# Softmax sums inverted once each through DRAM instead of as a 16-fold copy in SBUF, and down weights loaded in 11 pieces

## The chip, the core and the metric

The kernel runs on one core of a Trainium2 chip. The time is the device time of one execution in microseconds. Of three executions of the kernel before, the median is 1223.92 us (1220.72 to 1224.61).

## What is computed

One transformer layer, for 2 sequences of 1024 rows of 512 numbers, all in float32:

```
Q, K, V = x Wq^T + bq, x Wk^T + bk, x Wv^T + bv     # 32 query heads, 8 key/value heads, 16 wide
Q, K = rope(Q), rope(K)
w    = softmax(Q K^T / 4)                            # four query heads share one key head
x    = layernorm(x + (w V) Wo^T + bo)
h    = silu(x gate_w^T * gate_s) * (x up_w^T * up_s) # 1408 wide
x    = layernorm(x + (h down_w^T) * down_s)
```

What matters here is the division in the softmax. The kernel never divides the weights. It sums exp(score) x V and exp(score) over the keys, and at the end multiplies the first by the inverse of the second.

## The kernel before, in words

**Units, half-steps, iterations.** The attention is cut into 32 units (`UNITS`): one sequence, one half of 512 queries, and one key head g with its four query heads. Eight units (g from 0 to 7) make a quarter, q = 0 to 3. A unit has eight half-steps, one for each 128 keys. The loop over c (L698) does two half-steps per iteration, so a unit is four iterations and a quarter is 32; c runs from 0 to 127. Each iteration does, for the half-steps 2c and 2c+1:

- "A" products (`max_pass`, L340): scores of a unit that comes 12 half-steps later, for whose row maxima VectorE (DVE) reduces each bank (L356, eight in an iteration). `max_rows` (L359) then turns a unit's maxima, at the end of every iteration c = 1 modulo 4, with four small DVE operations and six DMAs by way of DRAM.
- "B" products (`exp_pass`, L378): the scores again, less the maxima, of which ScalarE (ACT) takes the exponential (L391, eight in an iteration).
- "V" products (`av`, L396): probabilities by V, where V is laid out with a column of ones beside each of its columns. So the accumulated result holds, for each of the four heads, sixteen rows of weighted values and, between them, sixteen equal rows of the sum of the weights.
- "F", at the head of an iteration, if there is some: one piece of other TensorE work from the list `fill`. That is first the projections of Q, K and V (up to iteration 20), and from then on the output projection and the feed-forward of the quarter before: two pieces `project` (L483), two `x1_turn` (L509), 22 `hidden` (L521) and four `down` (L568). `quarter` (L623) lists these 30 and gives the iteration `first` from which they may start.

The order of the products in an iteration is written out by hand in three lists: WITH_FILL (L683), NO_FILL (L686) and NO_A (L689, after the last A product). The order of instructions is the program's order on every engine. The products share seven banks of PSUM, handed out in turn.

**Hooks.** Before each V product `v_hook` (L692) runs what `after(k, f)` (L206) put off by k half-steps. `early` (L203) does the same at the head of an iteration. A piece that waits at a hook holds up all that comes behind it on its engine.

**The end of a unit.** `unit_out` (L413) runs with a unit's last V product, in the iteration after its last half-step. ScalarE copies the bank to `o`; two DMAs take the rows of values to `num` (L426) and the rows of sums to `den` (L427). Two units, with g even and odd, fill one `num` and one `den` of 128 rows. When the odd one is in, DVE inverts `den` in four strips of 128x128 (L432) and multiplies `num` by it (L437). For g = 7 this is placed at the next hooks, since the output projection of that quarter starts at iteration 32(q + 1) + 3; for other pairs it is placed two to four iterations later.

**The down weights.** Weights are rounded during the first 19 iterations and kept in a DRAM tensor `wsd`. The 11 slices of the down weights are fetched in one DMA at iteration 26 (L752), ahead of the first feed-forward weights and residuals. They are first read by `down`, at the end of the first quarter's feed-forward.

**The last quarter.** In quarters 0 and 1 the loop at L718 takes two pieces of `fill` in one slot where they would not all fit before the next quarter begins. Of quarter 2 two downs are kept (L770) and mixed with the projections of quarter 3 behind the loop. For the last quarter (`LASTQ`) the residuals come into a pool of five buffers (`fp5`), each when an output row of the quarter before has been stored (L597).

**The SP queue.** All DMAs are issued by SyncE (SP), in the order of the program. A DMA whose data isn't there yet holds up those behind it: KS, QH and QL of a later unit (`prep`, L325), the feed-forward weights `wt` (`ask_weights`, L458), the maxima's round trip.

Of the kernel before, what the change touches and what calls it, by code (L numbers as in the profile page):

```python
# [7 lines left out]
F32 = mybir.dt.float32  # L8
# [3 lines left out]
ALU = mybir.AluOpType  # L12
# [4 lines left out]
P = 128  # L17
B, T, D = 2, 1024, 512
HQ, HKV, HD = 32, 8, 16
G = HQ // HKV  # L20
E = 32
# [3 lines left out]
NF = INTER // P  # L25
# [3 lines left out]
HALF = 512  # L29
NH = T // HALF  # L30
# [9 lines left out]
QS = HKV * US  # L40
RING = 5
PIECES = 3 * NF
# [4 lines left out]
def attn_ffn_kernel(tc, x, wqkv, bqkv, wo, bo, rope, wg, wu, wd, gs, us, ds, out):  # L47
    nc = tc.nc

    def pool(name, bufs=1, **kw):  # L50
        return tc.alloc_tile_pool(name=name, bufs=bufs, **kw)
# [3 lines left out]
    dram2 = pool("dram2", 2, space=DRAM)  # L55
    ap1 = pool("ap1")
    ap2 = pool("ap2", 2)
# [20 lines left out]
    def leave(what):  # L78
        free.extend(held.pop(what, ()))
# [82 lines left out]
    wsd = dram.tile([PIECES, P, D], F32, name="wsd")  # L162
# [18 lines left out]
    def piece_round(i):  # L181
        w = SW.pop(i)
        SR[i] = sp4.tile([P, D], F32R, tag="sr", name="sr")
        nc.scalar.copy(SR[i], w)

        nc.vector.scalar_tensor_tensor(
            low, w.bitcast(I32), LOW, low, ALU.bitwise_and, ALU.bitwise_or
        )

    def piece_store(i):  # L190
        nc.sync.dma_start(out=wsd[i], in_=SR.pop(i).bitcast(F32))
# [8 lines left out]
        after(4, lambda: nc.vector.tensor_reduce(flag, flr, AX.X, ALU.max))  # L200

    later = {}
    early = {}  # L203
    now = [0]

    def after(n, f):  # L206
        later.setdefault(now[0] + n, []).append(f)
# [151 lines left out]
    def max_rows(u):  # L359


        neg = ap2.tile([P, TH, G], F32, tag="neg", name="neg")
        nc.vector.tensor_reduce(neg, MX.pop(u), AX.X, ALU.max, negate=True)
        mm = ap2.tile([P, G, 2, TH], F32R, tag="mm", name="mm")
        hi, lo = (mm[:, :, i, :].rearrange("p j t -> p t j") for i in range(2))
        nc.vector.tensor_copy(hi, neg)
        nc.vector.tensor_tensor(lo, neg, hi.bitcast(F32), ALU.subtract)
        mr = ap2.tile([P, E], F32, tag="mr", name="mr")
        nc.vector.transpose(mr, mm.bitcast(F32).rearrange("p j i t -> p (j i t)"))
        md = dram2.tile([E, P], F32, tag="md", name="md")  # L370
        for k in range(P // E):
            nc.sync.dma_start(out=md[:, k * E : (k + 1) * E], in_=mr[k * E : (k + 1) * E, :])
        rows = md.rearrange("(j i t) n -> i j (t n)", j=G, i=2)
        for i in range(2):
            nc.sync.dma_start(out=mts[u % 2][i : P : E, :].bitcast(F32), in_=rows[i])
# [16 lines left out]
            leave(("B", n, j))  # L392

    PV, PVN, NUM = {}, {}, {}

    def av(n, prob):  # L396
        u, kc = divmod(n, US)
# [15 lines left out]
    def unit_out(u):  # L413


        b, qh, g = UNITS[u]
        q = u // HKV
        o = ap1.tile([P, HALF], F32, tag="o", name="o")
        nc.scalar.copy(o, PV.pop(u))  # L419
        if g % 2 == 0:  # L420
            NUM[q, g // 2] = ap4.tile([P, HALF], F32, tag="num", name="num")
            NUM["den"] = ap1.tile([P, HALF], F32, tag="den", name="den")
        num, den = NUM[q, g // 2], NUM["den"]
        r0 = (g % 2) * G * HD
        rows = slice(r0, r0 + G * HD)
        nc.sync.dma_start(out=num[rows, :], in_=o[0:P:2, :])  # L426
        nc.sync.dma_start(out=den[rows, :], in_=o[1:P:2, :])  # L427
        if g % 2:
            c = now[0] // 2
            for k in range(TH):  # L430
                ns = slice(k * P, (k + 1) * P)
                f = lambda ns=ns: nc.vector.reciprocal(den[:, ns], den[:, ns])  # L432
                if g == HKV - 1:
                    after(k // 2 + 1, f)
                else:
                    early.setdefault(c + 2 + k // 2, []).append(f)
            f = lambda: nc.vector.tensor_tensor(num, num, den, ALU.mult)  # L437
            if g == HKV - 1:
                after(3, f)
            else:  # L440
                early.setdefault(c + 4, []).append(f)


    XQ, FP = {}, {}
    DONE = set()
    LASTQ = B * NH - 1

    def load_residual(q, t):
        b, qh = divmod(q, NH)
# [33 lines left out]
    def project(q, t):  # L483
        py = bank("py")
        for c in range(NC):
# [6 lines left out]
            )  # L492
        if q == LASTQ:
            row = XQ[q, t]
# [26 lines left out]
    def hidden(q, f, up):  # L521
# [13 lines left out]
        if not up:  # L535
            if f == 0:
# [8 lines left out]
            after(  # L545
                1 if q == LASTQ else 2,
                lambda: nc.vector.scalar_tensor_tensor(z, th, 1.0, z, ALU.add, ALU.mult),
# [4 lines left out]
        pus = FP["tmp"].tile(  # L552
            [P, HALF], F32, tag="pus" if q == LASTQ else "th", name="pus"
        )
        nc.scalar.mul(pus, p, ust[:, f : f + 1])  # L555

        def rest():
            nc.gpsimd.tensor_tensor(z, pus, z, ALU.mult)  # L558
            if q == LASTQ:
                nc.scalar.copy(hi, z)  # L560
# [7 lines left out]
    def down(q, t, f0=0, f1=NF):  # L568
# [14 lines left out]
        ys = fp1.tile([P, D], F32, tag="ys", name="ys")  # L583
        if q == LASTQ:
            nc.vector.tensor_tensor(ys, pd, dsb, ALU.mult)
# [8 lines left out]
        def store():  # L594
# [4 lines left out]
            for i in range(TH):  # L599
                if (q + 1, i) not in XQ and q < LASTQ and (q + 1, i) not in DONE:  # L600
                    if i <= t + (q + 1 == LASTQ):
# [19 lines left out]
    fill = [(0, f) for f in fill]  # L621

    def quarter(q):  # L623
        first = (q + 1) * QS // 2 + 3
        fs = [lambda t=t: (project(q, t), project(q, t + 1)) for t in (0, 2)]
        fs += [lambda t=t: (x1_turn(q, t), x1_turn(q, t + 1)) for t in (0, 2)]
        for f in range(NF):
            for up in (0, 1):
                fs.append(lambda a=(q, f, up): hidden(*a))
        downs = [(t, 0, NF) for t in range(TH)]  # L630
        if q == LASTQ:

            downs[:2] = [(0, 0, NF - 1), (1, 0, NF - 1), (0, NF - 1, NF), (1, NF - 1, NF)]
        for a in downs:
            fs.append(lambda a=a: down(q, *a))
        return [(first, f) for f in fs]
# [55 lines left out]
    def v_hook(n):  # L692
        now[0] = n
        for f in later.pop(n, ()):
            f()

    before = None
    for c in range(STEPS // 2):  # L698
        probs = {}

        pieces = [i for i in (2 * c - 4, 2 * c - 3) if 0 <= i < PIECES]
        for i in pieces:
            piece_round(i)
        if pieces:
            after(1, lambda ps=pieces: [(piece_store(i), piece_load(i + 4)) for i in ps])
        for f in early.pop(c, ()):
            f()
        alone = 2 * c + LEAD >= STEPS
        has_fill = bool(fill) and fill[0][0] <= c
        if c >= (STEPS - QS) // 2:  # L710
            has_fill = has_fill and len(fill) > 2
        for s in NO_A if alone else WITH_FILL if has_fill else NO_FILL:
            if s == "F":
                if has_fill:
                    fill.pop(0)[1]()
                    leave("F")

                    while c < (STEPS - QS) // 2 and (rest := len(fill) % PHASES) and QS // 2 - 1 - c % (QS // 2) < rest < DOWNS:  # L718
                        fill.pop(0)[1]()
                        leave("F")  # L720
                continue
            n = 2 * c + int(s[-1])
            if s[0] == "V":
                v_hook(n)
                if before is not None:
                    av(n - 2, before[n - 2])
                continue
            j, i = int(s[1]), "abc".index(s[2])
            if s[0] == "A":
                max_pass(n + LEAD, j, i)  # L730
                continue
            if i == 2 and n not in probs:
                probs[n] = ap3.tile([P, G, HALF], F32, tag="prob", name="prob")
            exp_pass(n, j, i, probs.get(n))
        before = probs
        u, s = divmod(2 * c + 1, US)
        if s == US - 1 and u + 3 < len(UNITS):
            prep(u + 3)
        if (2 * c + 1 + LEAD) % US == US - 1 and not alone:
            max_rows((2 * c + 1 + LEAD) // US)  # L740
        if c == QS // 2 - 10:
            low_flag()
        if c == QS // 2 - 6:
            sp4.release()
            qp4.release()
            qp2.release()
            qp1.release()
            fp1 = pool("fp1", side="right")
            fp2 = pool("fp2", 2, side="right")
            fp5 = pool("fp5", 5, side="right")  # L750
            wd_sb = fp1.tile([P, NF, D], F32R, name="wd_sb")
            nc.sync.dma_start(  # L752
                out=wd_sb.bitcast(F32), in_=wsd[2 * NF : PIECES].rearrange("f p n -> p f n")
            )
            FP["tmp"] = fp1
            ask_weights(RING - 1)
            for t in range(TH):
                load_residual(0, t)
            for q in range(B * NH - 1):
                fill.extend(quarter(q))  # L760
# [15 lines left out]
    n = 2 * STEPS  # L776
# [137 lines left out]
```

## Time and profile before

| what | value |
|---|---|
| median of three executions | 1223.92 us |
| the profiled execution | 1221.5 us, its span 1219.6 us |
| mean granted TensorE clock | 0.971 |
| DVE L356, reductions to maxima | 1024 of 682 ns |
| DVE L432, reciprocals 128x128 | 64, 893/896/954 ns (least, median, most) |
| DVE L437, num by den | 16 of 682 to 1158 ns |
| DMAs num<-o, den<-o | 32 each, 128 KB each |
| DMA wd_sb<-wsd | 1, 2816 KB, issued at 301.8 us |

The profile is that of one execution. "Busy" is the time in which an engine had an instruction in work; instructions that issue DMAs are not counted as busy. A busy TensorE is not TensorE at its peak. The chain of waits is followed back from the last instruction, at each step to what released it. The windows of the loop are named by their time in us from the start of the span. Their last columns are the granted TensorE clock (1.00 is full), the mean busy share of the 16 DMA engines and GB/s. In rows in order of time, the columns are the start, the duration, the engine (SPq is SP's queue) and the line; "[x <-y]" is idle time of the engine before the row, and what ended it.

### The profile page before, as it was taken

How to read it: one execution, taken by the hardware profiler on the slowest of the kernel's cores; microseconds unless marked ns; L12 is line 12 of the kernel's file. 1: busy time of each engine (PE TensorE's matmuls, PEld its weight loads, DVE VectorE, ACT ScalarE, POOL GpSimd, SP SyncE). 2: the span in 40 equal slices, each digit the busy share in tenths (PEclk: the TensorE clock that was granted, in tenths of full speed). 3: DMA queues.
4: the chain of work that ended last, by engine and by line, in shares of the span. 5: the costliest groups of instructions: out<-in, count | busy, mean ns of one | idle time of the engine just before them, and what ended most of it. 6: DMA issues, size and time to landing. Idle time of an engine off the chain costs nothing.

```text
span 1219.6 us, 22668 instructions
## 1 busy us (share of the span) xinstructions
PE 1159.8 (95%) x8784; PEld 599.9 (49%) x8784; DVE 872.3 (72%) x1492; ACT 702.7 (58%) x1300; POOL 352.4 (29%) x340
## 2 busy tenths in 40 slices
PE   7799999999999999999999999999899999999896
PEld 5344444444443554545444454446444454554585
DVE  4568898878877788876577878885758878742434
ACT  2016767656645677775445777774537777774251
POOL 3116362440103122223512222224412222226431
PEclk9769999999999999999999999999989999999899
DMA  5366877442611222222202222221312232111240
GB/s 162 105 190 223 271 244 252 148 175 61 202 45 62 80 80 80 80 85 65 88 28 88 80 80 80 80 80 53 114 37 75 85 95 81 46 54 53 95 122 37
DMA packets 82290, 126.80 MB, mean 104 GB/s; under 512 B 15873, under 2 KB 29442, under 8 KB 82050
## 3 DMA queue, kind: packets, MB, share of 16 engines
q1 hardware_dynamic: 82178, 125.30, 32.5%
q8 instruction: 71, 1.16, 0.4%
q14 instruction: 41, 0.34, 0.1%
HBM read 80.43 MB, written 36.44 MB: 96 GB/s over the span
## 4 chain that ended last, share of the span: by engine, by line
PE 72%; DVE 16%; POOL 4%; DMA 4%; issue 2%; ACT 1%; SPq 0%; POOLq 0%; DVEq 0%; ACTq 0%
PE pa L348 17%; PE pv L403 16%; PE pg L527 13%; PE pb L383 12%; DVE mx L356 8%; PE pq L256 5%; PE pd L574 4%; PE py L486 3%; DVE den L432 2%; DVE st L471 1%; POOL xq L591 1%; POOL ys L590 1%; ACT prob L391 1%; DMA den<-o 1%; POOL xq L481 1%
## 5 line engine op out<-in xcount | busy, mean ns | idle before, releaser
L356 DVE TENSOR_REDUCE mx<-pa 128x1 f32<-128x512 f32 x1024 | 644.6, 682 | 183.3 <-PE pa L348 130.5
L391 ACT ACTIVATE prob<-pb 128x512 f32<-128x512 f32 x1024 | 542.1, 600 | 239.9 <-PE pb L383 206.6
L348 PE MATMUL pa<-KS,QH 32*128 32x512 f32 x1024 | 361.2, 469 | 18.5 <-DVE mx L356 10.2
L348 PE MATMUL pa<-KS,QL 32*128 32x512 f32 x1024 | 336.3, 427 | 0.0
L383 PE MATMUL pb<-QH,KS 32*128 32x512 f32 x1024 | 309.4, 464 | 20.2 <-DVE mx L356 13.6
L383 PE MATMUL pb<-QL,KS 32*128 32x512 f32 x1024 | 277.5, 421 | 0.0
L403 PE MATMUL pv<-prob,va 128*32 128x512 f32 x2048 | 276.9, 612 | 0.0
L383 PE MATMUL pb<-mt,ones 32*128 32x512 f32 x1024 | 251.9, 403 | 0.0
L348 PEld LDWEIGHTS pa<-KS,QH 32*128 32x128 f32 x1024 | 155.7, 188 | 178.1 <-DVE mx L356 120.1
L558 POOL TENSOR_TENSOR z<-pus,z 128x512 f32<-128x512 f32 x44 | 56.3, 1279 | 445.4 <-ACT pus L555 418.3
L348 PEld LDWEIGHTS pa<-KS,QL 32*128 32x128 f32 x1024 | 167.1, 189 | 29.1 <-issue 19.0
L383 PEld LDWEIGHTS pb<-QL,KS 32*128 32x128 f32 x1024 | 131.2, 185 | 87.8 <-issue 85.8
L383 PEld LDWEIGHTS pb<-QH,KS 32*128 32x128 f32 x1024 | 131.0, 184 | 62.1 <-DVE mx L356 42.2
L527 PE MATMUL pg<-x1h,wt 128*128 128x512 f32 x352 | 146.3, 416 | 0.7 <-ACT x1h L516 0.7
L383 PEld LDWEIGHTS pb<-mt,ones 32*128 32x128 f32 x1024 | 138.5, 185 | 3.3
L527 PE MATMUL pg<-x1l,wt 128*128 128x512 f32 x352 | 139.2, 396 | 0.3 <-DVE x1l L517 0.3
L403 PEld LDWEIGHTS pv<-prob,va 128*32 128x32 f32 x2048 | 41.1, 108 | 94.2 <-issue 83.5
L527 PEld LDWEIGHTS pg<-x1h,wt 128*128 128x128 f32 x352 | 67.1, 191 | 38.0 <-issue 11.7
L256 PE MATMUL pq<-xT,wqkv_sb 128*128 128x512 f32 x160 | 77.9, 634 | 1.3 <-DVE mx L356 1.3
L527 PEld LDWEIGHTS pg<-x1l,wt 128*128 128x128 f32 x352 | 67.2, 191 | 12.8 <-DVE x1l L517 0.8
L574 PE MATMUL pd<-wd_sb,hh 128*128 128x512 f32 x176 | 69.9, 397 | 0.7 <-ACT o L419 0.7
L574 PE MATMUL pd<-wd_sb,hl 128*128 128x512 f32 x176 | 68.6, 390 | 0.0
(80 smaller groups left out, 968.9 us busy)
## 6 DMA issues: line engine op xcount, KB each, us to landing
wt<-wsd SPq DMA_DIRECT2D x88, 256.0 KB
KS<-kT SPq DMA_DIRECT2D x128, 128.0 KB
wsd<-sr SPq DMA_DIRECT2D x33, 256.0 KB
qT<-hi SPq DMA_DIRECT2D x16, 512.0 KB
qT<-lo SPq DMA_DIRECT2D x16, 512.0 KB
QH<-qT SPq DMA_DIRECT2D x32, 256.0 KB
QL<-qT SPq DMA_DIRECT2D x32, 256.0 KB
xs<-in_x_dram SPq DMA_DIRECT2D x16, 256.0 KB
```

The lines of the kernel that those rows point to most:

```text
L256: nc.tensor.matmul(pq, wqkv_sb[:, c, m * P : (m + 1) * P], XT[b, half][:, c, :], start=c == 0, stop=c == NC - 1,)
L348: nc.tensor.matmul(PA[n, j], (QH, QL)[i][u][r, t * P : (t + 1) * P], KS[u][r, half * HALF : (half + 1) * HALF], start=i == 0, stop=i == 1,)
L356: nc.vector.tensor_reduce(MX[u][:, t, j, half : half + 1], PA.pop((n, j)), AX.X, ALU.max)
L383: nc.tensor.matmul(PB[n, j], ones[r, :] if i == 2 else KS[u][r, kc * P : (kc + 1) * P], (QH[u], QL[u], mts[u % 2])[i][r, :], start=i == 0, ...
L391: nc.scalar.activation(prob[:, j, :], PB.pop((n, j)), AF.Exp, scale=SCALE)
L403: nc.tensor.matmul(PV[u][j * E : (j + 1) * E, :], vas[b][:, kc, g, :, :].rearrange("p d o -> p (d o)"), prob[:, j, :], start=done == 0, st ...
L432: f = lambda ns=ns: nc.vector.reciprocal(den[:, ns], den[:, ns])
L471: nc.vector.bn_stats(st, row)
L486: nc.tensor.matmul(py, NUM[q, c][:, t * P : (t + 1) * P], wo_sb[:, c, :], start=c == 0, stop=c == NC - 1,)
L527: nc.tensor.matmul(p, w[:, c, :], x1[:, c, :], start=c == 0 and k == 0, stop=c == NC - 1 and k == 1,)
L558: nc.gpsimd.tensor_tensor(z, pus, z, ALU.mult)
L574: nc.tensor.matmul(pd, h[:, f, t * P : (t + 1) * P], wd_sb[:, f, :], start=f == 0 and k == 0, stop=f == NF - 1 and k == 1,)
```

## The change

For all units but the last two (g = 6 and 7 of the last quarter, which keep the old way), `den` is no longer copied from `o` and inverted as it lies. Of the sixteen equal rows of each head one is stored to DRAM (`sd`, 4 x 512). From there 128 rows of 16 numbers are loaded (`rc`), DVE inverts these 2048 numbers once, they are stored to DRAM again (`rd`), and four DMAs spread each head's row over its sixteen rows of `den`. The stages follow each other by k half-steps: the load k after the unit's end, the inversion 2 later (k + 2), the spreading at 2k + 2, and for odd g the multiplication of `num` at 3k + 2. k is 1 for g = 7 and otherwise 2. All of them stand at hooks; `early` is gone.

The feed-forward of a quarter may start at iteration 32(q + 1) + 4 instead of + 3. The down weights are fetched in 11 DMAs of one slice, one at the end of each iteration from c = 36 to 46, instead of one DMA at c = 26.

```diff
--- before.py
+++ after.py
@@ -200,7 +200,6 @@
         after(4, lambda: nc.vector.tensor_reduce(flag, flr, AX.X, ALU.max))
 
     later = {}
-    early = {}
     now = [0]
 
     def after(n, f):
@@ -392,6 +391,7 @@
             leave(("B", n, j))
 
     PV, PVN, NUM = {}, {}, {}
+    LASTQ = B * NH - 1
 
     def av(n, prob):
         u, kc = divmod(n, US)
@@ -424,26 +424,45 @@
         r0 = (g % 2) * G * HD
         rows = slice(r0, r0 + G * HD)
         nc.sync.dma_start(out=num[rows, :], in_=o[0:P:2, :])
+        if q < LASTQ or g // 2 < HKV // 2 - 1:
+
+            sd = dram2.tile([G, HALF], F32, tag="sd", name="sd")
+            rd = dram2.tile([G, HALF], F32, tag="rd", name="rd")
+            rc = ap2.tile([P, G * HALF // P], F32, tag="rc", name="rc")
+            flat = "j (p n) -> (j p) n"
+            nc.sync.dma_start(out=sd, in_=o[1:P:E, :])
+
+            def inverse():
+                nc.vector.reciprocal(rc, rc)
+                nc.sync.dma_start(out=rd.rearrange(flat, n=G * HALF // P), in_=rc)
+
+            def spread():
+                for j in range(G):
+                    nc.sync.dma_start(
+                        out=den[r0 + j * HD : r0 + (j + 1) * HD, :],
+                        in_=rd[j : j + 1, :].to_broadcast([HD, HALF]),
+                    )
+
+
+            k = 1 if g == HKV - 1 else 2
+            after(k, lambda: nc.sync.dma_start(out=rc, in_=sd.rearrange(flat, n=G * HALF // P)))
+            after(k + 2, inverse)
+            after(2 * k + 2, spread)
+            if g % 2:
+                after(3 * k + 2, lambda: nc.vector.tensor_tensor(num, num, den, ALU.mult))
+            return
         nc.sync.dma_start(out=den[rows, :], in_=o[1:P:2, :])
         if g % 2:
-            c = now[0] // 2
             for k in range(TH):
                 ns = slice(k * P, (k + 1) * P)
-                f = lambda ns=ns: nc.vector.reciprocal(den[:, ns], den[:, ns])
-                if g == HKV - 1:
-                    after(k // 2 + 1, f)
-                else:
-                    early.setdefault(c + 2 + k // 2, []).append(f)
-            f = lambda: nc.vector.tensor_tensor(num, num, den, ALU.mult)
-            if g == HKV - 1:
-                after(3, f)
-            else:
-                early.setdefault(c + 4, []).append(f)
+                after(
+                    k // 2 + 1, lambda ns=ns: nc.vector.reciprocal(den[:, ns], den[:, ns])
+                )
+            after(3, lambda: nc.vector.tensor_tensor(num, num, den, ALU.mult))
 
 
     XQ, FP = {}, {}
     DONE = set()
-    LASTQ = B * NH - 1
 
     def load_residual(q, t):
         b, qh = divmod(q, NH)
@@ -621,7 +640,7 @@
     fill = [(0, f) for f in fill]
 
     def quarter(q):
-        first = (q + 1) * QS // 2 + 3
+        first = (q + 1) * QS // 2 + 4
         fs = [lambda t=t: (project(q, t), project(q, t + 1)) for t in (0, 2)]
         fs += [lambda t=t: (x1_turn(q, t), x1_turn(q, t + 1)) for t in (0, 2)]
         for f in range(NF):
@@ -703,8 +722,6 @@
             piece_round(i)
         if pieces:
             after(1, lambda ps=pieces: [(piece_store(i), piece_load(i + 4)) for i in ps])
-        for f in early.pop(c, ()):
-            f()
         alone = 2 * c + LEAD >= STEPS
         has_fill = bool(fill) and fill[0][0] <= c
         if c >= (STEPS - QS) // 2:
@@ -738,6 +755,8 @@
             prep(u + 3)
         if (2 * c + 1 + LEAD) % US == US - 1 and not alone:
             max_rows((2 * c + 1 + LEAD) // US)
+        if 0 <= (f := c - QS // 2 - 4) < NF:
+            nc.sync.dma_start(out=wd_sb[:, f, :].bitcast(F32), in_=wsd[2 * NF + f])
         if c == QS // 2 - 10:
             low_flag()
         if c == QS // 2 - 6:
@@ -749,9 +768,6 @@
             fp2 = pool("fp2", 2, side="right")
             fp5 = pool("fp5", 5, side="right")
             wd_sb = fp1.tile([P, NF, D], F32R, name="wd_sb")
-            nc.sync.dma_start(
-                out=wd_sb.bitcast(F32), in_=wsd[2 * NF : PIECES].rearrange("f p n -> p f n")
-            )
             FP["tmp"] = fp1
             ask_weights(RING - 1)
             for t in range(TH):
```

## The prediction

> **What bounds the kernel now.** I read the page first, then the chain of waits, then the loop cut into iterations (each runs from the first V product of one iteration to that of the next), then DVE's and SP's rows in order of time.
>
> ```profile
> PE 1159.8 (95%) x8784; PEld 599.9 (49%) x8784; DVE 872.3 (72%) x1492; ACT 702.7 (58%) x1300; POOL 352.4 (29%) x340
> ...
> PE 72%; DVE 16%; POOL 4%; DMA 4%; issue 2%; ACT 1%; SPq 0%; POOLq 0%; DVEq 0%; ACTq 0%
> PE pa L348 17%; PE pv L403 16%; PE pg L527 13%; PE pb L383 12%; DVE mx L356 8%; PE pq L256 5%; PE pd L574 4%; PE py L486 3%; DVE den L432 2%; DVE st L471 1%; POOL xq L591 1%; POOL ys L590 1%; ACT prob L391 1%; DMA den<-o 1%; POOL xq L481 1%
> ```
>
> On average TensorE bounds, but a sixth of the chain is DVE: reductions (L356) and 2.4% (29 us) reciprocals (L432). Where DVE matters is told only by iteration. Windows of iterations 48 to 52, with feed-forward work in each (columns: window, length, then busy us and instructions of PE, PEld, DVE, ACT, POOL):
>
> ```profile
> 469.70:476.90 7.20, 7.20 (x69) 3.65 (x65) 5.07 (x9) 5.48 (x11) 3.14 (x3) 1.00 0.53 176
> 476.90:484.10 7.20, 7.20 (x70) 3.67 (x66) 6.58 (x14) 5.34 (x10) 0.04 (x1) 1.00 0.06 22
> 484.10:492.40 8.30, 7.82 (x71) 3.71 (x67) 7.48 (x12) 5.10 (x10) 3.13 (x3) 1.00 0.22 67
> 492.40:499.80 7.40, 7.40 (x70) 3.74 (x66) 6.72 (x12) 5.38 (x10) 0.04 (x1) 1.00 0.30 79
> 499.80:507.00 7.20, 7.20 (x72) 3.67 (x71) 5.09 (x9) 5.52 (x11) 3.12 (x3) 1.00 0.50 164
> ```
>
> 7.2 us is TensorE's pace (eight pg products take 2.04, the attention part about 5.15). Only the window with three of the four reciprocals is longer, by 1.1, the next by 0.2: DVE is late, banks stay full, TensorE waits. Iterations 30 to 35, the first four without such work, the last two with a projection of 7.08 us:
>
> ```profile
> 325.20:331.00 5.80, 5.80 (x61) 2.99 (x63) 5.19 (x9) 3.84 (x8) 0.00 (x0) 1.00 0.03 6
> 331.00:336.70 5.70, 5.70 (x59) 2.92 (x56) 5.09 (x9) 4.06 (x9) 0.00 (x0) 1.00 0.00 0
> 336.70:342.50 5.80, 5.80 (x62) 2.96 (x59) 5.20 (x9) 4.63 (x10) 0.00 (x0) 1.00 0.67 208
> 342.50:351.40 8.90, 6.76 (x63) 2.96 (x60) 8.20 (x13) 4.64 (x9) 0.00 (x0) 0.99 0.04 15
> 351.40:365.90 14.50, 14.50 (x79) 6.35 (x76) 7.66 (x16) 4.24 (x8) 0.00 (x0) 0.89 0.02 3
> 365.90:378.80 12.90, 12.59 (x79) 5.20 (x75) 7.81 (x15) 4.24 (x8) 5.76 (x6) 1.00 0.27 83
> ```
>
> A plain iteration is DVE's: eight reductions of 0.682 with 0.04 between them give 5.76, against 5.15 that TensorE needs. There every DVE microsecond counts in full: iteration 33, with the four reciprocals, is 3.1 longer, and the first projection is 1.6 longer than the second.
>
> **Reciprocals out.** 64 of 896 ns become 4 (the last pair keeps its own) and 30 of 128x16. One small one is not in the trace: an eighth of 896 is 0.11; the 128x16 cast and subtraction take 0.18 and 0.20; 0.11 + 0.20 is the upper end. I take 0.2, 0.24 with its gap. DVE's busy time falls by 60 x 0.896 - 30 x 0.2 = 48 to about 824, but it counts only as follows.
>
> - Feed-forward iterations, eight pairs: windows 41-43, 49-51, 57-59, 73-75, 81-83, 89-91, 105-107, 113-115 lie above three times 7.18 by 1.33, 1.35, 1.35, 1.34, 1.33, 1.35, 1.34 and 1.71, together 11.1. The new work (a small one in each iteration c = 2 mod 4, the product of 0.68 in every eighth) leaves DVE below 7.18: all of it is gained. A ninth pair (1076 to 1085 us) meets no more reductions: nothing.
> - Iterations with projections of Q, K, V (TensorE 8.78): pairs at 9-11 and 17-19 cost 1.7 and 0.24. The first product moves to iteration 12, where DVE already has 8.8 of 8.92: -0.5. Gain 1.4.
> - Plain iterations 21 to 34, two pairs: 8 x 0.936 = 7.5, less four small ones, 1.0: 6.5.
> - The turns at 65 and 97: four reciprocals 3.75, less one small: 3.5 each, 7.0.
>
> **The four transfers.** For a group's last unit they are one half-step apart (about 2.1 and 3.6 us in turn), otherwise two. Durations come from SP's rows and the chain:
>
> ```profile
> 272.75 1.72 SPq L372 DMA_DIRECT2D md<-mr  x4
> 275.53 1.15 SPq L375 DMA_DIRECT2D mt<-md  x2
> 278.74 0.34 SPq L198 DMA_DIRECT2D fl<-red  x1
> 286.05 0.23 SPq L199 DMA_DIRECT2D flr<-fl  x1
> ```
> ```profile
> 341.44 2.86 DMA den<-o
> 344.32 1.76 DVE den L432 x2
> ```
>
> Before, den landed 2.86 after its issue, and DVE waited 0.67 for it. The nearest rows to the 64-byte pieces are md<-mr (128-byte pieces; the read-back was issued 1.1 after the last write) and fl<-red (4-byte pieces: 7.3). The Trainium skill, "DMA: Bandwidth & Descriptors" (Specifications), speaks against this change: below 512 bytes a transfer is a read-modify-write and off line rate. By the row md<-mr the store rd takes about 1.6, by fl<-red, the slow end of such a rule, 7.3. I take 1.6, since 64 is nearer to 128 than to 4 and the total is only 8 KB. Then, for the turn at 33: o at 340.9, sd landed 343.7, rc landed 346.7 (2.96, as flr<-fl), inversion at iteration 34's first hook, 348.3 plus about 1 of DVE's lag; rd landed about 351.2; four spreads at 0.5 each on SP; den landed about 356. The product stands at iteration 35's first hook, 354 plus 1 of lag: DVE waits about 1.2. Behind it are that iteration's reductions, and TensorE for their banks. In return the old wait of 0.7 goes. Three turns: -3.6 + 2.1 = -1.5; the bounds are 0 and 3 x 6.9 (rd as slow as fl). In the other units each gap is a whole iteration (5.8 to 8.8) and hides even 7.3, but for about 1 on SP. 190 more DMAs at 0.3 to 0.6 are SP's; behind a unit's four spreads (2.2) comes the next unit's KS, QH, QL, which needs 2.6 of issue and 3.6 to land of two iterations (11.5 or more): covered.
>
> **Feed-forward one iteration later** (first is +4). Each quarter gets one more plain iteration (5.76) and one fewer slot. Two quarters then do three downs in one slot, where two and one were done. Windows 60 and 61 (15.33, 11.75) give way to 5.16 + 3 x 5.2 = 20.8: 5.76 + 20.8 - 27.1 = -0.5, so +1.0 gained in all; the reason is that DVE's wait for POOL's sum (L471) comes once less. The x1 transposes now meet the maxima's four small operations and four statistics in one iteration (10.1 of DVE against about 7.2 of TensorE) with a light one after it; the sum is that of before: -0.4 for each of three, -1.2. The third quarter has no downs to merge: a plain iteration loses 0.6 against TensorE's pace, and its second down moves from iteration 126 to 127. From there runs a chain that the trace shows from 1106 to 1147: sum on POOL, statistics, normalisation (2.10), store, load of a residual (3.36), bias on POOL (1.28), next sum. The down ends about 6.5 before the last V product instead of 10.1; norm 7.6, store issued 8.4, landed 11.1, residual 14.5, bias 15.9: 9.4 after that product, where POOL's next sum now starts 6.7 after it. -2.7; bounds 0 (the chain has slack) and -5.9 (a whole iteration).
>
> **Down weights in pieces.** The transfer of 2816 KB at 301.8 is over long before iteration 60; no wait on the chain is for it or behind it. The pieces land from iteration 36 to 46. Zero; bounds +1 and -1 (KS behind it or pieces before wt).
>
> **Sum.** 11.1 + 1.4 + 6.5 + 7.0 - 1.5 + 1.0 - 1.2 - 0.6 - 2.7 = 21.0. The profiled execution took 1221.5 (span 1219.6 and 1.9 around it): 1200.5. It was 2.4 below the median of three, 1223.9, so for a median I say 1203.
>
> **Rivals.** (1) *The turn takes the gain*: small pieces are slow both ways (rd and rc each about 7.3), and the three multiplications stand still. From 8.2 per turn (24.6, the sum without the new waits, over three) the change is slower than before; both at 7.3, rc would be 4.3 later with 1 to 2 to spare and rd 5.7 later: 1.2 + 3 + 5.7 = 9.9 a turn, 1229. For it: fl<-red and the rule; against it: md<-mr. 7%. (2) *Half of it given back*: the plain stage turns out TensorE's or ACT's, the turns wait 4, and the end loses 5.9: -6 - 8.4 - 3.2, 1220 at worst, 1212 at half. For it: the chain's last stage; against it: DVE's share of the plain windows. 17%. (3) *More is gained*: no wait at the turns and no loss at the end, 1203 - 6.3 = 1197, with the half clock of 3.4 us at the turns gone too, 1193. 10%. My own: 66%.
>
> **Numbers.** Forecast 1203. From 1195 to 1214 holds my case, most of (3) and the better half of (2). Faster by over 0.3% (about what a measurement of this kernel can tell) 0.90, within 0.03, slower 0.07.
>
> **What would show it.** Right: iterations 41-43, 49-51 and so on all 7.2; L432's successor x4 and DVE near 824; iterations 33 and 34 near 5.8 to 7.2; DVE waiting for den about 1 us at each turn; the last stage some 3 us longer. Wrong: DVE waiting for rc or den in the middle of a group, windows over 7.3 in feed-forward iterations, or TensorE waiting over 5 us at iterations 35, 67, 99.

## The result, and the profile after

Of twelve executions of each kernel, the changed kernel's take 1223.62 us in the median (1220.68 to 1228.54), those of the kernel before 1224.26. The ratio is 0.999, 95% interval 0.9972 to 1.0008. The change makes no difference that can be measured. The forecast, 1203 with a range from 1195 to 1214, was wrong. The profiled execution after took 1222.9 us, its span is 1221.0, against 1219.6 before.

The page of the changed kernel, its first part and its chain:

```profile
PE 1161.7 (95%) x8784; PEld 605.7 (50%) x8784; DVE 829.6 (68%) x1462; ACT 700.7 (57%) x1300; POOL 354.0 (29%) x340
...
PE 79%; DVE 10%; DMA 5%; POOL 3%; issue 2%; ACT 1%; SPq 0%; POOLq 0%; DVEq 0%
PE pv L403 18%; PE pa L347 17%; PE pg L546 14%; PE pb L382 13%; DVE mx L355 6%; PE pq L255 6%; PE pd L593 5%; PE py L505 4%; DVE st L490 1%; POOL xq L500 1%; POOL ys L609 1%; POOL xq L610 1%; PE pv L306 1%; DMA fl<-red 1%; ACT prob L390 1%
```

The reciprocals have gone as planned: DVE is busy 829.6 us instead of 872.3 (824 was forecast), and its share of the chain falls from 16% to 10%. But the chain did not get shorter; TensorE took the share over, 79% instead of 72%. Page shares say where the chain now runs, not that anything was saved.

Iterations 49 to 51, the same three that the prediction showed (window, length, then busy us and instructions of PE, PEld, DVE, ACT, POOL, then granted clock, DMA share, GB/s):

```profile
475.40:482.60 7.20, 7.20 (x68) 3.64 (x64) 5.87 (x13) 4.97 (x10) 3.17 (x3) 1.00 0.04 11
482.60:489.80 7.20, 7.20 (x71) 3.68 (x67) 5.77 (x11) 5.36 (x10) 0.04 (x1) 1.00 0.31 79
489.80:497.00 7.20, 7.20 (x72) 3.67 (x71) 5.09 (x9) 5.01 (x10) 3.13 (x3) 1.00 0.24 61
```

Here the forecast holds to 0.1 us: 8.30 and 7.40 have become 7.20. Iterations 33 to 36, the first turn, do the opposite:

```profile
343.50:349.30 5.80, 5.80 (x60) 2.95 (x57) 5.15 (x9) 4.16 (x9) 0.00 (x0) 1.00 0.02 3
349.30:355.60 6.30, 6.30 (x59) 3.02 (x56) 5.83 (x14) 4.12 (x9) 0.00 (x0) 1.00 0.04 8
355.60:374.50 18.90, 16.69 (x82) 7.31 (x79) 6.98 (x12) 4.67 (x9) 0.00 (x0) 0.82 0.21 64
374.50:387.30 12.80, 12.48 (x76) 5.15 (x72) 7.71 (x15) 4.74 (x9) 5.76 (x6) 1.00 0.10 31
```

The two plain iterations are as short as forecast. The first projection takes 18.9, against 12.8 for the second and 14.5 before. Two things are to be seen in its row: TensorE stands still for 2.2 (18.9 less 16.69), and its granted clock is 0.82 (the kernel before had 0.89 there). SP's and DVE's rows at that turn:

```profile
350.12 2.46 SPq L371 DMA_DIRECT2D md<-mr  x4
353.67 1.06 SPq L374 DMA_DIRECT2D mt<-md  x2
354.78 0.43 SPq L437 DMA_DIRECT2D rd<-rc  x1
356.29 1.70 SPq L441 DMA_DIRECT2D den<-rd  x4
```
```profile
351.18 0.24 DVE L436 RECIPROCAL rc<-rc 128x16 f32<-128x16 f32 x1
...
359.58 0.69 DVE L452 TENSOR_TENSOR num<-num,den 128x512 f32<-128x512 f32 x1 [2.80 <-DMA den<-rd]
```

The inverse is ready at 351.42, but its store is issued at 354.78. Ahead of it on SP stand the six DMAs of the maxima, the last two of which wait for the first four to land. The store itself was quick: 1.5 from its issue to that of the first spread (2.7 and 1.6 at the other two turns). DVE then waits 2.80 for den (3.39 and 2.34 at the other two). TensorE stands still, and after that it has half its clock: the record of the clock in the trace has 6.8 us of half clock from 362.2, and there lies the projection, which is all TensorE's. The kernel before had half clock at its turns too: 3.4, 3.4 and 6.8 us, against 6.8, 6.8 and 3.4 now.

Iterations 61 and 62, the merged downs, and DVE's rows in the second (the first of three statistics stands just ahead of them):

```profile
561.60:581.90 20.30, 20.30 (x129) 14.51 (x125) 5.81 (x13) 6.00 (x11) 8.37 (x8) 1.00 0.02 4
581.90:598.40 16.50, 13.23 (x82) 7.99 (x78) 7.38 (x16) 4.83 (x9) 11.10 (x12) 0.79 0.05 9
```
```profile
583.78 0.66 DVE L490 BATCH_NORM_STATS2 st<-xq 128x6 f32<-128x512 f32 x1
584.47 0.18 DVE L491 BATCH_NORM_AGGREGATE mv<-st 128x2 f32<-128x6 f32 x1
584.57 0.66 DVE L490 BATCH_NORM_STATS2 st<-xq 128x6 f32<-128x512 f32 x1
587.53 0.18 DVE L491 BATCH_NORM_AGGREGATE mv<-st 128x2 f32<-128x6 f32 x1 [2.30 <-POOL xq L500]
```

Three downs in one slot take 20.3, as worked out. But the next window is 16.5 instead of 11.8. The third statistic waits 2.30 for POOL's normalisation L500, which does not make its input: it reads the `mv` of the first down, and there are two buffers for three.

By regions, from the same boundaries in both traces (start of the first V product of the iteration; the last V product ends at 1116.1 and 1117.0). The extra plain iteration of each turn, 5.76, is on a line of its own:

| region | forecast | measured |
|---|---|---|
| up to iteration 1 | 0 | +0.8 |
| 1 to 20 | -1.4 | -2.0 |
| 21 to 32 | -3.0 | +2.2 |
| three turns | -3.0 each | +1.7, +1.9, -0.3 |
| x1 transposes | +0.4 each | +0.1, 0, 0 |
| feed-forward of quarters 0 and 1 | -4.0 each | -5.7, -4.2 |
| downs of quarters 0 and 1 | -6.3 each | -0.5, -2.2 |
| from there to the last V product | -8.2 | -8.2 |
| after it | +2.7 | +0.4 |
| three plain iterations | +17.3 | +17.3 |
| sum | -21.0 | about +1.4 |

Of the 5.7 gained in the feed-forward of quarter 0, 1.5 is a stretch of half clock that the execution before had at 395.6. From iteration 1 to the last V product the changed kernel has 44 us of half clock in all, the kernel before 20. As an estimate, those 24 us more cost at most 12, of the 22 by which the sum missed.

### The profile page after: what moved, and what is told of

It is laid out like the page before. It is cut to its first block, busy times and chain, and to the rows that moved or that the text cites. A ratio compares the mean times of both kernels' runs of the same rounds, so it can differ in the third digit from the quotient of the medians.

```text
span 1221.0 us, 22849 instructions
## 1 busy us (share of the span) xinstructions
PE 1161.7 (95%) x8784; PEld 605.7 (50%) x8784; DVE 829.6 (68%) x1462; ACT 700.7 (57%) x1300; POOL 354.0 (29%) x340
## 4 chain that ended last, share of the span: by engine, by line
PE 79%; DVE 10%; DMA 5%; POOL 3%; issue 2%; ACT 1%; SPq 0%; POOLq 0%; DVEq 0%
PE pv L403 18%; PE pa L347 17%; PE pg L546 14%; PE pb L382 13%; DVE mx L355 6%; PE pq L255 6%; PE pd L593 5%; PE py L505 4%; DVE st L490 1%; POOL xq L500 1%; POOL ys L609 1%; POOL xq L610 1%; PE pv L306 1%; DMA fl<-red 1%; ACT prob L390 1%
## 5 line engine op out<-in xcount | busy, mean ns | idle before, releaser
L382 PEld LDWEIGHTS pb<-mt,ones 32*128 32x128 f32 x1024 | 142.5, 186 | 3.1
```

Source lines behind the costliest of these rows:

```text
L382: nc.tensor.matmul(PB[n, j], ones[r, :] if i == 2 else KS[u][r, kc * P : (kc + 1) * P], (QH[u], QL[u], mts[u % 2])[i][r, :], start=i == 0, ...
```

## Experiments

Each was run beside the kernel before on the same chip in five rounds. Since the medians of the kernel before differ by up to 3 us from set to set (1222.96 to 1226.22), the ratio is what is compared. All keep the whole computation.

**The later start alone.** Edit to the kernel before:

```diff
-        first = (q + 1) * QS // 2 + 3
+        first = (q + 1) * QS // 2 + 4
```

> The kernel before with one edit: a quarter's feed-forward may start one iteration later (+4). Theory (the loss of the change sits in three kinds of place: DVE waiting for den at the turns, the three merged downs, the first plain stage): here only the merged downs lose, about 5 us in each of two quarters, and the end 2 to 3, while the extra plain iteration gives DVE room after the four old reciprocals, -1 to -2 a turn: 6 to 10 slower, about 1231. Rival (the shift alone carries the whole give-back, the transfers are innocent): about 20 slower, 1244.

Measured: 1239.46 against 1222.96, 1.0129 (1.0106 to 1.0151), 16.5 slower. That is between the two expectations, and so it refuted the theory's sum: a loss had been missed. It shows in SP's and DVE's rows at the second turn of this kernel:

```profile
608.08 0.38 SPq L597 DMA_DIRECT2D out_dram<-xq  x1
608.50 0.43 SPq L452 DMA_DIRECT2D xq<-in_x_dram  x1
609.03 0.40 SPq L597 DMA_DIRECT2D out_dram<-xq  x1
611.55 0.33 SPq L452 DMA_DIRECT2D xq<-in_x_dram  x1
611.97 0.38 SPq L597 DMA_DIRECT2D out_dram<-xq  x1
614.12 0.33 SPq L452 DMA_DIRECT2D xq<-in_x_dram  x1
614.54 0.52 SPq L426 DMA_DIRECT2D num<-o  x1
615.11 0.59 SPq L427 DMA_DIRECT2D den<-o  x1
```
```profile
618.34 1.76 DVE L432 RECIPROCAL den<-den 128x128 f32<-128x128 f32 x2 [4.35 <-DMA den<-o]
```

Merging the downs also put their three stores at one hook, just ahead of the turn's num and den. The second and the third residual load each stand until an earlier store has landed (over 2 us after the row ahead of it), and num and den wait behind them all. DVE waits 4.35 (0.62 in the kernel before).

**The turns left alone.** Edit to the changed kernel:

```diff
-        if q < LASTQ or g // 2 < HKV // 2 - 1:
+        if g // 2 < HKV // 2 - 1:
...
-        first = (q + 1) * QS // 2 + 4
+        first = (q + 1) * QS // 2 + 3
```

> The changed kernel with the groups g = 6 and 7 of every quarter left on the old path and the start of the feed-forward back at +3; the other pairs and the down weights as changed. Theory: the 13 us gained in iterations with other TensorE work stay, turns, downs and end are as before; the first plain stage gives 0 to +2: 1210 to 1213. Rival (the small transfers and the longer SP queue cost everywhere): 1218 or more.

Measured: 1209.00 against 1222.96, 0.9885 (0.9864 to 0.9906). As the theory said. The four transfers of 12 pairs, with the down weights in pieces, gain about 14, with 144 of the 180 DMAs that they add in all (six more for each of 24 units); the longer queue does not cost everywhere.

**The down weights in one DMA.** Edit to the changed kernel: the fetch of all 11 slices at iteration 26 again, none later.

> The changed kernel with the down weights in one DMA at iteration 26 again. Theory: no row after iteration 34 changes; at iterations 26 to 32 the large transfer stands ahead of the spreading of den, 0 to +4: 1223 to 1228. Rival (the pieces on SP's queue take what was gained): faster by 5, 1219.

Measured: 1228.71 against 1222.96, 1.0041 (1.0026 to 1.0055). Against 0.999 for the changed kernel that is about 6 slower. In its trace the window of iteration 28 takes 15.7 instead of 8.5: the spreads are issued at 312.7, behind the large transfer, five weights and four residuals, and DVE waits 9.15 for den:

```profile
312.72 2.33 SPq L441 DMA_DIRECT2D den<-rd  x4
```
```profile
319.12 0.71 DVE L452 TENSOR_TENSOR num<-num,den 128x512 f32<-128x512 f32 x1 [9.15 <-DMA den<-rd]
```

So the pieces, which the prediction put at nothing, are worth about 6 here, because spreads now stand behind that transfer that weren't there before.

**The turn's stages earlier.** Edit to the changed kernel:

```diff
-            after(k + 2, inverse)
-            after(2 * k + 2, spread)
+            after(2 if k == 1 else 4, inverse)
+            after(3 if k == 1 else 6, spread)
```

> The changed kernel with the stages of a group's last unit at half-steps 1, 2, 3 and 5 instead of 1, 3, 4 and 5, so that the store of the inverse and the four spreads stand ahead of the DMAs of the maxima on SP. Theory: DVE's wait for den at the turns (2.8 us in the trace) falls below 1, TensorE does not stand still before the projections and keeps its full clock there: 4 to 5 us a turn, 1209 to 1213; the downs and the first plain stage stay as they are. Rival (the turn loses by the plain iteration, not by the wait): within 3 us of the changed kernel; or DVE now waits for rc as long as it did for den: the same.

Measured: 1216.53 against 1222.96, 0.9933 (0.9909 to 0.9956): 7 faster than the changed kernel, half of what was expected. The first turn gained 4.3 (its projection 14.6 instead of 18.9). At the second and third the wait moved to rc, as the rival had it: the windows of iterations 65 and 97 grew from 5.8 to 10.7 and 8.9, since the stores of the downs, seen above, now hold up sd and rc:

```profile
612.84 0.25 DVE L436 RECIPROCAL rc<-rc 128x16 f32<-128x16 f32 x1 [4.64 <-DMA rc<-sd]
```

One thing in the expectation is not so: only the store rd moved ahead of the maxima's DMAs. The spreads, one half-step later, still stand behind them.

**Four buffers for the statistics.** Edit to the changed kernel: st, mv and rs from a pool of four instead of `fp2`.

> The changed kernel with four buffers instead of two for the statistics (st, mv, rs). Theory: three downs in one slot put three statistics at one hook; the third waits for a buffer until POOL has finished a normalisation of 2.1 us, TensorE stands still 3.3 us and then runs at half clock. With four buffers the windows of iterations 62 and 94 fall from 16.5 and 16.3 to about 12: 4 to 5 us each, 1214 to 1217. Rival (DVE waits for POOL's sum, which more buffers don't hasten): no more than 1 us.

Measured: 1217.01 against 1226.22, 0.9915 (0.9884 to 0.9945). Its windows of iterations 61 and 62:

```profile
562.40:582.70 20.30, 20.30 (x126) 14.53 (x122) 5.81 (x13) 6.00 (x11) 8.35 (x8) 1.00 0.03 7
582.70:594.50 11.80, 10.69 (x82) 6.27 (x78) 7.40 (x16) 4.83 (x9) 11.11 (x11) 1.00 0.06 13
```

16.5 became 11.8, with the full clock. That window is now what the prediction had assumed. The cause is the buffer.

**The later start, mended.** The kernel before with the later start, the four buffers, and the stores of merged downs two half-steps earlier:

```diff
-        after(1 if q == LASTQ else 2 if now[0] >= STEPS else 5, store)
+        after(1 if q == LASTQ else 2 if now[0] >= STEPS else 3 if q < LASTQ - 1 and t < 3 else 5, store)
```

> The kernel before with the later start (+4), four buffers for the statistics, and the stores of the merged downs two half-steps earlier, so that they and the residual loads stand on SP well ahead of num and den. Theory: of the 16.5 us that the later start alone cost, about 9 are the third statistic and 5 to 7 are den queued behind three stores and loads at the second and third turn; only the end (2 to 3) and 1 or so more remain: 1224 to 1228. Rival (it is the extra plain iteration itself): still 10 or more slower, 1233.

Measured: 1225.46 against 1226.22, 0.9993 (0.9978 to 1.0008). Nothing is left of the 16.5. The window of iteration 62 is 11.8 instead of 15.6, and DVE's wait for den at the second turn is 0.36 instead of 4.35. The later start costs nothing measurable in itself; it cost a missing buffer and a place in SP's queue. The two mends were not tried on the kernel before without the later start; there the window of iteration 62 is 11.8 and the wait 0.62 already.

**Stores and stages.** The variant with the earlier stages and those earlier stores; two buffers for the statistics.

> The variant with the earlier turn stages (1216.5, 0.9933 of the kernel before) and the stores of the merged downs two half-steps earlier; the statistics keep two buffers. Theory: its windows of iterations 65 and 97 (10.7 and 8.9, DVE waiting for rc behind three stores and loads on SP) fall to 5.8, 3 to 5 us each, with 62 and 94 still at 15.6 or more: 0.986 to 0.989. Rival (rc is late for its own sake): unchanged, 0.993.

Measured: 1207.71 against 1224.62, 0.9865 (0.9844 to 0.9886). The windows of iterations 65 and 97 fell to 5.8 and 6.7; rc was late because of the queue.

**All three.** The changed kernel with the buffers, the stores and the stages.

> The changed kernel with three edits: four buffers for the statistics, the stores of the merged downs two half-steps earlier, and the stages of a group's last unit at half-steps 1, 2, 3 and 5. Theory: each turn's wait for rc or den falls below 1.5 us and the downs cost no more than before; with the 13 us of the other pairs this gives 1199 to 1204. Rival (a wait always comes back elsewhere): not below the variant that leaves the turns alone, 1209.

Measured: 1206.78 against 1226.22, 0.9855 (0.9825 to 0.9886), 19.4 faster. That is about what had been forecast for the change, and short of what was expected of this variant. The wait of DVE at the turns fell to 1.8, 2.0 and 0.9 only, since the spreads still stand behind the maxima's DMAs. Its first turn has the projection at full clock:

```profile
357.30:371.90 14.60, 13.41 (x79) 5.86 (x76) 6.98 (x12) 4.68 (x9) 0.00 (x0) 1.00 0.28 83
```

It came out level with the variant before it, although it also mends the downs (windows 62 and 94 fell from 15.6 to 11.8 in both quarters). The two ran beside different sets of the kernel before, and the intervals overlap: they can't be ranked by their times.

**The first loads later.** The variant with the turns left alone, and the first five weights and four residuals asked for at the end of iteration 28 instead of 26.

> The variant with the turns left on the old path (1209.0) and, besides, the first feed-forward weights and residuals asked for at the end of iteration 28 instead of 26. Theory: at iterations 27 and 28 the spreads of den and the next unit's KS no longer queue behind nine transfers of 256 KB; the window of iteration 28 falls from 8.9 to about 6.2 and the two after it by 0.6: 1205 to 1206. Rival (the wait moves to the next unit's transfers): 1208 to 1210.

Measured: 1207.45 against 1226.22, 0.9839 (0.9808 to 0.9870), against 0.9885 without it; the two intervals just overlap, and the windows tell more. The changed kernel's window of iteration 28, SP's rows ahead of it and DVE's row in it:

```profile
310.30:318.80 8.50, 6.70 (x59) 2.99 (x56) 5.96 (x10) 4.99 (x10) 5.42 (x4) 0.94 0.73 249
```
```profile
303.26 0.43 SPq L437 DMA_DIRECT2D rd<-rc  x1
303.74 2.33 SPq L482 DMA_DIRECT2D wt<-wsd  x5
306.11 2.11 SPq L471 DMA_DIRECT2D xq<-in_x_dram  x4
308.26 3.41 SPq L441 DMA_DIRECT2D den<-rd  x4
312.15 2.82 SPq L330 DMA_DIRECT2D KS<-kT  x4
```
```profile
315.66 0.81 DVE L452 TENSOR_TENSOR num<-num,den 128x512 f32<-128x512 f32 x1 [1.95 <-DMA KS<-kT]
```

And SP's rows in the variant with later loads:

```profile
303.27 0.43 SPq L437 DMA_DIRECT2D rd<-rc  x1
304.80 1.69 SPq L441 DMA_DIRECT2D den<-rd  x4
309.48 1.70 SPq L330 DMA_DIRECT2D KS<-kT  x4
```

Nine transfers of 256 KB stood between rd and den. DVE waited at the product, which reads num and den alone; the profile puts the wait down to KS, which was issued behind den and came last. The window was 8.5 to 8.9. With the nine gone it is 5.9, and the next is 5.8 instead of 6.9 to 7.8.

**Four edits.** All three and the later loads.

> The variant with three edits (1206.8 beside 1226.2 for the kernel before) and the first feed-forward weights and residuals asked for at the end of iteration 28. Theory: the windows of iterations 28 and 29 fall from 9.2 and 8.4 to 6 each as they did on the old turns; 4 to 6 faster than without: a ratio to the kernel before of 0.980 to 0.982, about 1203. Rival (the first turn then waits for what came later): no gain over 0.9855.

Measured: 1196.04 against 1224.62, 0.9778 (0.9751 to 0.9805), 28.6 faster, more than expected. It is the fastest version found. Its loop has one stretch of half clock, 3.4 us, where the changed kernel's has 44 us. It ran beside the same set as "Stores and stages", and is 11.7 faster than that variant.

## Why the prediction was wrong, point by point

A gain of 21.0 was forecast, and the two profiled executions differ by 1.4 the other way. By the table the missing 22 lie in three terms: the turns (12.3), the downs (9.9) and iterations 21 to 32 (5.2). The other terms came out 5 better than forecast.

- **Reciprocals out: right.** 1.33 to 1.71 us a pair are gained in feed-forward iterations, each window at 7.2. A small reciprocal takes 0.242 us instead of the 0.2 assumed. In iterations 1 to 20 the gain was 2.0 instead of 1.4, since the first product hid in its iteration after all (8.92 before and after).
- **"In the other units each gap is a whole iteration ... and hides even 7.3": failed at iteration 28.** What failed is the place on SP: the four spreads were issued 5.0 after the store of the inverse, behind the first loads, and den was late for the product. With that, and a stretch of half clock from 290.5, iterations 21 to 32 gave +2.2 instead of -3.0. With the loads moved, iterations 28 and 29 fell by 5. Iterations 24 and 25 take 1.2 and 1.5 less in the variant with the earlier turn, which is the same program up to there, and without a stretch of half clock; why the clock fell in one execution and not in the other stays open.
- **"DVE waits about 1.2" at the turns: failed, and its price more than its size.** The store rd took 1.5, 2.7 and 1.6 to the issue of the first spread, where 1.6 was assumed and 7.3 feared. So the row md<-mr was the right neighbour; a delay like that of fl<-red, which the rule of small transfers had made thinkable, is in none of the three. The rival built on it had the right place and the wrong cause. What I left out was SP's order: the maxima's round trip of an iteration's end stands ahead of a store at the next hook. DVE waited 2.3 to 3.4, TensorE stood still 1.7 to 2.7, and the projection then ran at half clock for 6.8, 6.8 and 3.4 us. Measured against forecast: 4.7, 4.9 and 2.7 lost. That the turn cost this is shown by the variants with the earlier stages: where rd stands ahead of the maxima's DMAs, and rc is not held up, the first projection takes 14.3 to 14.6 instead of 18.9.
- **"Three downs in one slot ... the wait comes once less": failed, 5.8 and 4.1 lost.** I counted DVE's waits for POOL's sum, and not the buffers that three statistics at one hook need.
- **What the merge does to the stores was not in the prediction at all.** In the changed kernel the long stages hid most of it; in the variant that brought the turn forward and left the stores where they were, the windows of iterations 65 and 97 grew by 4.9 and 3.1; in the kernel with the later start alone they are 4.2 and 2.5 longer than before.
- **Down weights in pieces, "zero": wrong for this kernel.** Undone within the change it costs about 6. In the kernel before no spread stood behind the transfer, so that the pieces alone would have gained nothing of this kind there; that was not run.
- **The end: right in mechanism.** From the last V product to the first feed-forward product of the last quarter it is 32.7 instead of 30.5, +2.3 (forecast +2.7), but 1.8 of it came back behind; why is not known.
- **The rivals.** The one called "half of it given back" (17%) came nearest in time, 1220 at worst, yet it too had the turns' wait and not the clock or the buffers. That the change would make no difference had been given 0.03. Of the signs of being wrong one came, a wait in the middle of a group (iteration 28); TensorE never waited 5 us at a turn, and the loss was there all the same.

The gain was real, and was given back at other places by four new waits: a queue position at the turns, one at iteration 28, one ahead of the second and third turn, and a buffer. Three of them are waits for one's place behind other DMAs, where I had priced only the transfers themselves. Half clock of TensorE followed on each of them in one trace or another, and made it worse than its own length.

## What to carry to other kernels

When a step is moved or cut into stages, write down for each stage what is issued ahead of it on its queue at that hook, with what those DMAs wait for; the duration of the transfer alone is the smaller part. When work is merged into one slot, count everything that it puts at one hook: buffers, statistics, stores. And a stall of TensorE just ahead of a stretch that is all TensorE's (here 1.3 to 2.7 us) is to be priced with the half clock that may follow it.

## What the runs showed of the hardware that was not expected

The half clock came after stalls, and not after each. Two kernels, that with three edits and that with four, had nearly the same second turn: DVE's wait for den 1.96 and 2.00, TensorE still for 1.28 and 1.33. The first ran its projection at full clock and took 14.7; the other had a stretch of 3.4 us at half clock and took 16.5, 1.8 more, which is about half of 3.4.

In the traces the stretches within the loop are 3.4, 6.8, 10.2 or 13.7 us, multiples of 3.4. More than that: in each of the twelve traces all changes of the clock lie on one grid of 3.413 us, to within 0.002, and only the place of the grid differs from trace to trace. This fits the Trainium skill, "TensorE: Matmul & The Clock Gate" (Part 1), by which the gate judges activity in free-running windows of about 3.4 us. It would also explain why kernels that are alike in an iteration differ there by 1.5.

But it doesn't tell when the clock falls. Two neighbouring windows of the grid at that second turn, first with four edits, then with three (length, then busy us of PE, PEld, DVE, ACT, POOL, then granted clock, DMA share, GB/s):

```profile
609.32:612.73 3.41, 2.55 (x18) 1.69 (x19) 3.33 (x7) 1.18 (x3) 0.00 (x0) 1.00 0.00 0
612.73:616.14 3.41, 3.41 (x5) 1.35 (x4) 0.47 (x1) 0.99 (x3) 0.00 (x0) 0.50 0.76 223
```
```profile
618.26:621.67 3.41, 2.13 (x25) 0.79 (x25) 1.45 (x4) 1.57 (x3) 0.00 (x0) 1.00 0.12 19
621.67:625.08 3.41, 3.31 (x20) 1.99 (x21) 2.95 (x5) 2.03 (x4) 0.00 (x0) 1.00 0.12 35
```

The same part of the skill gives half clock after an idle window. Here TensorE was busy for 2.55 of 3.41 us in the window ahead of the half clock, and in the other kernel for 2.13 without losing its clock. So a stall much shorter than a window was enough in one place, and more idle time in a window was not in another. What decides is not shown by these runs.
